# Head-by-head copies out of PSUM in the chunked gated delta rule of a two-layer network

## Chip, core and metric

The kernel runs on one core of a Trainium2 chip. The metric is the device time of one execution in microseconds (us), as the median of several runs. Profiles are of one execution each.

## What is computed

The reference is a two-layer network on x of shape (2, 1024, 256): causal attention with 32 heads of 8, a gated FFN with int8 weights, then a gated delta rule with 16 heads of 128, then an FFN with sign weights; after each a residual and a layer norm. The change touches only the delta rule. Its core, per head and time step, is:

```python
err = jnp.einsum('bhvk,bhk->bhv', S, kt) - vt
S = at[..., None, None] * S - bt[..., None, None] * err[..., None] * kt[:, :, None, :]
o = jnp.einsum('bhvk,bhk->bhv', S, qt)
```

with S a 128 x 128 state for each of 2 x 16 heads, 1024 steps, k scaled by 128 ** -0.5, and q, k, v each made by a projection of x, a causal convolution over 4 steps and a silu. The outputs o are normalised over a head's 128 values, gated, and projected back to 256 columns.

## The kernel before

The recurrence is worked in chunks of 128 time steps. A half sequence has 512 steps (HT), so four chunks (HC = 4); two heads are taken together (HP = 2, a head pair), which makes 8 pairs (NS). With 4 half sequences there are 32 pair steps `i`, each of 4 chunks: 128 chunks in all.

For one chunk of one pair, `recur` (line 488) does this for both heads h, whose results stand side by side in one PSUM tile (a "bank" of 512 float32 columns, made by `bank`, line 129; head h has columns 128h to 128h+127, the slice `r`):

- **rows**, lines 517 and 521: `pr` = transpose of v plus k times the state M, two products for each head, started by the transpose and added to by the second. The second is left out where there is no state yet.
- line 523: ScalarE copies both heads' rows, 256 columns, into SBUF as `prs`.
- **solution**, line 529: `pw` = the chunk's inverted triangular matrix `lt` times `prs`, one product for each head.
- line 531: ScalarE copies both heads' solutions, 256 columns, into SBUF as `wc`.
- **new state**, line 541: `pm` = `kc` times `wc`; VectorE makes the new M from it and the old one (lines 545 and 547).
- **outputs**, lines 554 and 555: `po` = q times the old M plus `at` times `wc`; ScalarE copies them out as `o` (line 558).

All of these products are of float32 data and have 128 output columns for each head. `pr`, `pw`, `pm` and `po` come in turn from one pool of two banks, `pools["c"]`.

Beside the recurrence of pair i, `merge` (line 663) mixes in generators for other work: `keys(i + 4)` (the projection, convolution and Gram matrix of k), `others` (the same for q and v, products of k and q), `rest_of` (gates), `levels` and `blocks` (the inversion of the triangular matrices), `finish` (normalisation and output projection, called through `tail`), and in the last pair steps the FFN of the second layer. Each generator yields numbers that say how much TensorE time has been spoken for, and `merge` takes the one that is furthest behind. That gives the order in which instructions are recorded. When the program is built the framework's scheduler (line 1446, `schedule_with_timeline_sim=True`) places each engine's instructions once more, by their dependences and its own idea of their times; it also puts in the semaphore waits. On the chip each engine takes its instructions strictly in the placed order. A wait of a product therefore holds up all that stands behind it on TensorE.

TensorE's other work in this stage, by line: projections (lines 790 to 792, `pp`, 512 columns, and `pf`, 256 columns), Gram matrices (253, 404), transposes (395, 458), and the levels of the inversion (325 to 380). ScalarE's other work: lines 209, 213 and 223 (convolution and silu), 343 to 381 (levels), 422, 449 and 460 (gates and normalisation).

Of the kernel before, what the change touches and what calls it, by code (L numbers as in the profile page):

```python
# [11 lines left out]
F32 = mybir.dt.float32  # L12
# [8 lines left out]
P = 128  # L21
# [10 lines left out]
HP = 2  # L32
# [56 lines left out]
def delta_rule(  # L89
# [13 lines left out]
    nc = tc.nc  # L103
# [6 lines left out]
    pools = {}  # L110
# [18 lines left out]
    def bank(pool, tag, name):  # L129
        return pool.tile([P, HT], F32, name=name, tag=tag)  # L130
# [47 lines left out]
    def place(i):  # L178

        return divmod(i, NS)  # L180
# [307 lines left out]
    def recur(i):  # L488

        hi, s = place(i)  # L490
        ge = halves[hi]["ge"]
        M = state[s] if hi % 2 else None
        wo = []
        for part in range(2):
            t = pools["late"].tile([P, HP, E], F32R, name=f"wo{part}", tag=f"wo{part}", bufs=1)
            nc.sync.dma_start(
                out=t.bitcast(F32),
                in_=w1d["o", part][s * HP * P : (s + 1) * HP * P, :].rearrange("(h p) e -> p h e", p=P),
            )
            wo.append(t)  # L500

        def tail():
            while tails:
                w = next(tails[0], None)
                if w is not None:
                    return w
                tails.pop(0)
            return 0.0

        lt = st[i]["lt"]  # L510
        o = pools["late"].tile([P, HC, HP, P], F32, name="o", tag="o")
        for c in range(HC):
            t = slice(c * P, (c + 1) * P)
            pr = bank(pools["c"], "c", "pr")
            for h in range(HP):
                r = slice(h * P, (h + 1) * P)
                nc.tensor.matmul(
                    pr[:, r], lhsT=st[i]["v", h][:, t], rhs=ident, start=True, stop=(M is None), is_transpose=True
                )
                if M is not None:  # L520
                    nc.tensor.matmul(pr[:, r], lhsT=st[i]["k", h][:, t], rhs=M[:, r], start=False, stop=True)
            prs = pools["late"].tile([P, HP * P], F32, name="prs", tag="prs")
            nc.scalar.copy(prs, pr[:, 0 : HP * P])  # L523
            yield 0.65
            yield tail()
            pw = bank(pools["c"], "c", "pw")
            for h in range(HP):
                r = slice(h * P, (h + 1) * P)
                nc.tensor.matmul(pw[:, r], lhsT=lt[:, h * HC + c, :], rhs=prs[:, r], start=True, stop=True)  # L529
            wc = pools["late"].tile([P, HP * P], F32, name="wc", tag="wc")  # L530
            nc.scalar.copy(wc, pw[:, 0 : HP * P])  # L531
            yield 0.45
            yield tail()
            Mn = None
            if hi % 2 == 0 or c < HC - 1:
                pm = bank(pools["c"], "c", "pm")
                keep = dict(tag="S", bufs=NS) if c == HC - 1 else dict(tag="M")
                Mn = pools["late"].tile([P, HP * P], F32, name="M", **keep)
                for h in range(HP):
                    r = slice(h * P, (h + 1) * P)  # L540
                    nc.tensor.matmul(pm[:, r], lhsT=st[i]["kc", h][:, c, :], rhs=wc[:, r], start=True, stop=True)  # L541
                for h in range(HP):
                    r = slice(h * P, (h + 1) * P)
                    if M is None:
                        nc.vector.tensor_copy(Mn[:, r], pm[:, r])
                    else:
                        nc.vector.scalar_tensor_tensor(
                            Mn[:, r], M[:, r], ge[:, s * HP + h, c : c + 1], pm[:, r], ALU.mult, ALU.add
                        )
            po = bank(pools["c"], "c", "po")  # L550
            for h in range(HP):
                r = slice(h * P, (h + 1) * P)
                if M is not None:
                    nc.tensor.matmul(po[:, r], lhsT=st[i]["q", h][:, t], rhs=M[:, r], start=True, stop=False)  # L554
                nc.tensor.matmul(  # L555
                    po[:, r], lhsT=st[i]["at", h][:, t], rhs=wc[:, r], start=(M is None), stop=True
                )
            nc.scalar.copy(o[:, c, :, :].rearrange("p h t -> p (h t)"), po[:, 0 : HP * P])  # L558
            M = Mn
            if i == last and c in (HC // 2 - 1, HC - 1):  # L560
                tails.append(finish(i, wo, o, range(c + 1 - HC // 2, c + 1)))
            yield 1.3
            yield tail()
        state[s] = M
        if i < last:
            tails.append(finish(i, wo, o, range(HC)))
# [114 lines left out]
    for i in range(-AHEAD, last + 1):  # L681
# [19 lines left out]
        if i >= 0:  # L701
            parts.append((recur(i), RECUR))
# [747 lines left out]
```

## Time and profile before

| what | us |
|---|---|
| median of 3 runs (2094.62 to 2099.72) | 2094.68 |
| the profiled execution | 2099.4 |
| its span, first to last instruction | 2097.7 |
| the stretch with the recurrence in it, from 837 to 2033 us | 1196 |
| TensorE busy in that stretch | 1127.43 |
| VectorE busy in it | 965.91 |
| ScalarE busy in it | 658.57 |
| GpSimd busy in it | 501.71 |

The profile names engines PE (TensorE's products), PEld (its weight loads, which run beside products), DVE (VectorE), ACT (ScalarE), POOL (GpSimd) and SP (the queue that issues most DMAs). A group's row reads: line, engine, operation, output<-inputs, shapes, count | busy time in us, mean ns of one | idle time of the engine just before them, and what ended it. A float32 product with 128 columns shows as two MATMUL records, so the 256 products of line 529 are x512; a float32 transpose shows as one. Consecutive MATMUL records overlap: four of them that start 0.11 us apart show as one row of 0.60 us. The waits view lists who waited for whom, with total us, number of times and the longest.

### The profile page before, as it was taken

What the parts mean: (1) busy time and instruction counts of PE and PEld (TensorE: products, weight loads), DVE (VectorE), ACT (ScalarE), POOL (GpSimd) and SP (SyncE); (2) the same over time, 40 slices, a digit from 0 to 9 for tenths busy, and PEclk for the clock granted to TensorE, in tenths of its full rate; (3) what the DMA queues carried; (4) which work ended last, traced back from release to release, by engine and by line L of the source; (5) the groups of instructions that cost most, each with busy time, mean ns of one, the idle gap of its engine ahead of it and who ended that gap; (6) DMA issues with size and microseconds to landing.
All of it is one profiled execution on the core that took longest, in us unless ns stands there. A gap on an engine that the chain in (4) does not pass through costs nothing.

```text
span 2097.7 us, 48705 instructions
## 1 busy us (share of the span) xinstructions
PE 1905.9 (91%) x18656; PEld 1498.2 (71%) x18656; DVE 1611.1 (77%) x3878; ACT 1131.9 (54%) x2349; POOL 762.8 (36%) x1217
## 2 busy tenths in 40 slices
PE   4989999999988887899999999999999999999996
PEld 2545555555555786788888888888888888787885
DVE  5756666877747996587788878888898888978587
ACT  2355566576655345555555555655564565555543
POOL 1243333331123322144363443444345344344331
PEclk9899999999999899999999999999999999999999
DMA  7454443442132421443444444443444343443110
GB/s 222 144 164 144 144 131 126 142 134 68 51 75 61 133 64 35 127 126 91 119 121 115 124 118 115 107 120 107 121 131 119 113 118 107 137 118 107 32 41 31
DMA packets 313514, 230.90 MB, mean 110 GB/s; under 512 B 139649, under 2 KB 278657, under 8 KB 313281
## 3 DMA queue, kind: packets, MB, share of 16 engines
q1 hardware_dynamic: 299472, 210.80, 34.6%
q10 hardware_dynamic: 9632, 10.76, 1.6%
q0 software_dynamic: 4176, 6.23, 1.2%
q8 instruction: 147, 2.41, 0.5%
q14 instruction: 87, 0.70, 0.1%
HBM read 172.95 MB, written 51.87 MB: 107 GB/s over the span
## 4 chain that ended last, share of the span: by engine, by line
PE 50%; DVE 19%; ACT 6%; DMA 5%; issue 4%; SPq 1%; POOL 1%; POOLq 0%; DVEq 0%; ACTq 0%
PE pp L790 4%; PE pp L792 4%; PE pp L791 4%; PE ps L1110 4%; PE av L1131 3%; PE ps L1058 3%; DVE q L216 2%; PE pkq L404 2%; DVE at L247 2%; PE pw L529 2%; PE pm L541 2%; DVE k L216 2%; PE pkk L253 2%; PE po L555 2%; PE p L380 2%
## 5 line engine op out<-in xcount | busy, mean ns | idle before, releaser
L1067 DVE TENSOR_REDUCE mx<-ps 128x4 f32<-128x1024 f32 (+1 forms) x320 | 344.7, 1111 | 133.5 <-PE ps L1058 91.9
L1114 ACT ACTIVATE es<-ps 128x512 f32<-128x512 f32 (+1 forms) x608 | 314.8, 577 | 135.3 <-PE ps L1110 128.7
L1110 PE MATMUL ps<-qT,kT 128*128 128x512 f32 (+3 forms) x768 | 221.1, 369 | 17.9 <-ACT es L1114 15.8
L1058 PE MATMUL ps<-kT,qT 128*128 128x512 f32 x576 | 203.2, 428 | 23.3 <-DVE mx L1067 16.9
L1110 PEld LDWEIGHTS ps<-qT,kT 128*128 128x128 f32 x768 | 130.9, 189 | 106.2 <-ACT es L1114 53.7
L216 DVE SCALAR_TENSOR_TENSOR k<-pp,cw,k 128x511 f32<-128x511 f32 (+2 forms) x192 | 141.8, 740 | 31.0 <-ACT k L209 19.9
L1058 PEld LDWEIGHTS ps<-kT,qT 128*128 128x128 f32 x576 | 102.5, 194 | 85.7 <-DVE mx L1067 51.9
L1131 PE MATMUL av<-es,vaug 128*32 128x512 f32 (+3 forms) x1536 | 161.7, 501 | 0.0
L216 DVE SCALAR_TENSOR_TENSOR v<-pp,cw,v 128x511 f32<-128x511 f32 (+2 forms) x192 | 141.2, 738 | 13.1 <-ACT halos L213 8.5
L416 POOL TENSOR_TENSOR q<-q,dg 128x512 f32<-128x512 f32 x64 | 82.2, 1285 | 184.5 <-ACT pt L460 31.6
L216 DVE SCALAR_TENSOR_TENSOR q<-pp,cw,q 128x511 f32<-128x511 f32 (+2 forms) x192 | 139.2, 733 | 11.0 <-ACT q L209 9.4
L740 POOL TENSOR_TENSOR wfl<-wf,wfh 128x256 fp32r<-128x256 f32 x80 | 58.4, 733 | 208.3 <-ACT wfh L828 165.2
L1117 POOL TENSOR_SCALAR_AFFINE_SELECT es<-es 128x512 f32<-128x512 f32 x128 | 80.3, 636 | 146.9 <-ACT es L1114 146.7
L529 PE MATMUL pw<-prs,lt 128*128 128x128 f32 x512 | 84.8, 288 | 23.4 <-ACT prs L523 23.3
L555 PE MATMUL po<-wc,at 128*128 128x128 f32 x512 | 98.4, 279 | 2.1 <-ACT wc L531 1.2
L763 POOL TENSOR_TENSOR om<-om 128x8 f32<-128x8 f32 x93 | 20.3, 218 | 213.7 <-DVE om L756 113.8
L529 PEld LDWEIGHTS pw<-prs,lt 128*128 128x128 f32 x512 | 70.7, 194 | 33.2 <-ACT prs L523 29.7
L558 ACT COPY o<-po 128x256 f32<-128x256 f32 x128 | 47.6, 372 | 79.3 <-PE po L555 78.4
L242 POOL TENSOR_SCALAR_AFFINE_SELECT d<-col 128x512 f32<-128x512 f32 x64 | 51.2, 812 | 105.6 <-DVE at L247 96.7
L554 PE MATMUL po<-M,q 128*128 128x128 f32 x448 | 87.6, 278 | 0.0
L828 ACT CAST wfh<-wf 128x256 fp32r<-128x256 f32 x80 | 32.3, 406 | 101.6 <-DMA wf<-in_w1k 28.6
L531 ACT COPY wc<-pw 128x256 f32<-128x256 f32 x128 | 47.5, 371 | 72.7 <-PE pw L529 71.7
(305 smaller groups left out, 5646.1 us busy)
## 6 DMA issues: line engine op xcount, KB each, us to landing
da<-dec SPq DMA_DIRECT2D x64, 256.0 KB
wk<-w1k SPq DMA_DIRECT2D x64, 256.0 KB
wq<-w1q SPq DMA_DIRECT2D x64, 256.0 KB
wv<-w1v SPq DMA_DIRECT2D x64, 256.0 KB
dg<-dec SPq DMA_DIRECT2D x64, 256.0 KB
wg<-w1g SPq DMA_DIRECT2D x64, 256.0 KB
wo<-w1o SPq DMA_DIRECT2D x64, 256.0 KB
ad<-avs ACTq DMA_DIRECT2D x32, 256.0 KB
```

The costliest lines, as they stand in the source:

```text
L216: nc.vector.scalar_tensor_tensor(acc[:, d:], pp[:, 0 : HT - d], cw[:, n, hd, KS - 1 - d : KS - d], acc[:, d:], ALU.mult, ALU.add)
L529: nc.tensor.matmul(pw[:, r], lhsT=lt[:, h * HC + c, :], rhs=prs[:, r], start=True, stop=True)
L554: nc.tensor.matmul(po[:, r], lhsT=st[i]["q", h][:, t], rhs=M[:, r], start=True, stop=False)
L555: nc.tensor.matmul(po[:, r], lhsT=st[i]["at", h][:, t], rhs=wc[:, r], start=(M is None), stop=True)
L790: nc.tensor.matmul(out, lhsT=lhi, rhs=rhi, start=k0, stop=False)
L791: nc.tensor.matmul(out, lhsT=lhi, rhs=rlo, start=False, stop=False)
L792: nc.tensor.matmul(out, lhsT=llo, rhs=rhi, start=False, stop=k1)
L1058: anchor["mm"] = nc.tensor.matmul(ps[:, j - j0, :].rearrange("p (g k) -> p g k", k=P), lhsT=q_, rhs=kT[:, :, j * P : (j + 1) * P], start=T ...
L1067: nc.vector.tensor_reduce(mx[:, it, j0 // 2, :], ps[:, 0:n, :].rearrange("p j (g k) -> p g j k", k=P), AX.XY, ALU.max)
L1110: nc.tensor.matmul(ps[:, g - g0, :], lhsT=kT[:, g, jb * P : (jb + 1) * P], rhs=qT[:, i0 : i0 + w], start=True, stop=True,)
L1114: exps.append(nc.scalar.activation(es[:, g0 : g0 + n, 0:w], ps, AF.Exp, scale=D ** -0.5))
L1131: mm = nc.tensor.matmul(av[ROW * g : ROW * (g + 1), i0 - ih * 512 : 512], lhsT=vaugs[b][:, jb, kv, :], rhs=es[:, g, 0:w], start=(jb == 0), ...
```

## The change

Both copies of a chunk are cut in two. Each head's half of the rows is copied as soon as its own products are recorded, before the other head's products are recorded; the same is done for the solutions. The tiles `prs` and `wc` are made before the loops. Products, their operands and their number are the same.

```diff
+
             pr = bank(pools["c"], "c", "pr")
+            prs = pools["late"].tile([P, HP * P], F32, name="prs", tag="prs")
             for h in range(HP):
                 r = slice(h * P, (h + 1) * P)
                 nc.tensor.matmul(
...
                 if M is not None:
                     nc.tensor.matmul(pr[:, r], lhsT=st[i]["k", h][:, t], rhs=M[:, r], start=False, stop=True)
-            prs = pools["late"].tile([P, HP * P], F32, name="prs", tag="prs")
-            nc.scalar.copy(prs, pr[:, 0 : HP * P])
+                nc.scalar.copy(prs[:, r], pr[:, r])
             yield 0.65
             yield tail()
             pw = bank(pools["c"], "c", "pw")
+            wc = pools["late"].tile([P, HP * P], F32, name="wc", tag="wc")
             for h in range(HP):
                 r = slice(h * P, (h + 1) * P)
                 nc.tensor.matmul(pw[:, r], lhsT=lt[:, h * HC + c, :], rhs=prs[:, r], start=True, stop=True)
-            wc = pools["late"].tile([P, HP * P], F32, name="wc", tag="wc")
-            nc.scalar.copy(wc, pw[:, 0 : HP * P])
+                nc.scalar.copy(wc[:, r], pw[:, r])
             yield 0.45
             yield tail()
```

In the changed kernel the rows' transposes stand on line 519, the state's products on 523, the two copies on 524 and 532, the solution on 531, the new state on 542 and the outputs on 555 and 556.

## The prediction

> **What bounds the kernel now.** I read the busy shares by engine first, then the stretch with the recurrence, then TensorE's waits in it, then one such wait in order of time.
>
> ```profile
> span 2097.7 us, 48705 instructions
> PE 1905.9 (91%) x18656; PEld 1498.2 (71%) x18656; DVE 1611.1 (77%) x3878; ACT 1131.9 (54%) x2349; POOL 762.8 (36%) x1217
> PE   4989999999988887899999999999999999999996
> ACT  2355566576655345555555555655564565555543
> 837.00:2033.00 1196.00, 1127.43 (x13684) 994.88 (x13684) 965.91 (x2654) 658.57 (x1392) 501.71 (x847) 0.98 0.40 111
> ```
>
> The 128 chunks lie between 837 and 2033 us (first and last row of line 523 in the trace). There TensorE is busy 1127 of 1196 us (94%), VectorE 81%, ScalarE 55%, and the granted clock is 0.98. TensorE's in-order stream sets the end: what adds idle time to it is paid, unless another wait shrinks for it.
>
> ```profile
> PEld pw L529 <- ACT prs L523: 29.7, 29, 9.0
> PEld pm L541 <- ACT wc L531: 14.6, 22, 0.9
> PEld pp L790 <- DVE q L216: 10.7, 14, 1.6
> PEld p L360 <- ACT n L356: 5.9, 6, 2.7
> PEld pp L790 <- DVE k L216: 4.4, 6, 1.1
> PEld po L555 <- ACT wc L531: 2.2, 5, 0.5
> ```
>
> These are waits in that stretch. The two copies cost 29.7 + 14.6 + 2.2 = 46.5 us in 56 places. One of 9.0 us is the first chunk's, where the copy itself was late behind VectorE; without it 37.5 us in 55 places. All other waits of the weight loads there sum to 74.1 us.
>
> ```profile
> 1077.01 0.60 PE L529 MATMUL pw<-prs,lt 128*128 128x128 f32 x4
> ...
> 1077.65 0.37 ACT L531 COPY wc<-pw 128x256 f32<-128x256 f32 x1 [2.40 <-PE pw L529]
> ...
> 1078.07 0.52 PEld L541 LDWEIGHTS pm<-wc,kc 128*128 128x128 f32 x4 [0.65 <-ACT wc L531]
> 1078.07 0.71 PE L541 MATMUL pm<-wc,kc 128*128 128x128 f32 x4 [0.46 <-ACT wc L531]
> ```
>
> A bare stop looks like this. Four records 0.11 us apart from 1077.01 would let the next go at 1077.45; it goes at 1078.07, so 0.62 us of TensorE is lost: 0.20 until the copy starts, 0.37 of copy, 0.05 back.
>
> **The change, part by part.** Products: same kind and number, so no TensorE work is added or removed. Copies: 256 of 256 columns (372 ns each) become 512 of 128 columns. No row shows a 128-column copy out of PSUM. Nearest rows:
>
> ```profile
> L523 ACT COPY prs<-pr 128x256 f32<-128x256 f32 x128 | 47.6, 372 | 37.8 <-PE pr L521 23.6 <-DVE pi L300 7.3 <-PE pr L517 6.0
> L213 ACT COPY halos<-pp 128x3 f32<-128x3 f32 x96 | 14.6, 152 | 0.0
> L338 ACT COPY X<-px 32x512 f32<-32x512 f32 x16 | 9.2, 577 | 0.2
> ```
>
> The price lies between 152 (3 columns) and 372 ns (256); the slopes between these rows, 0.80 and 0.87 ns a column, give 261 to 270, and I take 265. ScalarE then does 512 x 0.265 - 256 x 0.372 = +40 us, going from 659 to 699 us of 1196; it has over 40% idle there, so by itself this costs nothing. Were a ScalarE instruction always queued ahead, its neighbours would be 0.16 us later per chunk and copy kind.
>
> Whether halves overlap is decided by the waits. The built order of the changed program has, in one chunk (lines of the changed kernel):
>
> ```
> L523 pr<-M,k      first head
> ...
> L519 pr<-ident,v  second head   waits ScalarE
> L523 pr<-M,k      second head
> L531 pw<-prs,lt   first head
> ...
> L531 pw<-prs,lt   second head   waits ScalarE
> L542 pm<-wc,kc    first head
> L542 pm<-wc,kc    second head   waits ScalarE
> ```
>
> The second head's transpose into `pr` reads nothing that ScalarE made just then; its semaphore value is that of the first head's copy out of the same bank. That holds in 126 of 128 chunks with a wait on that transpose itself, and for `pw` in 127. So a half's copy does not stand beside the other half's products: the product waits for the copy. Where the old chunk made TensorE stop at two points (before `pw`, before `pm`), the new one can stop at three: before the second `pr`, the second `pw`, the second `pm`. The first `pw` and first `pm` no longer wait.
>
> A rule of the Trainium skill speaks against the change here: "PSUM — Partial Sum Buffer", section "PSUM bank collisions raise a hardware error", says that two engines must not touch one PSUM bank (within 32 partitions) at once, even at disjoint columns, and that access is to be guarded by bank and not by address. The trace of before cannot show this, since its copies start after both heads' products. By the rule the waits must stay and the sum below holds; without it the first rival's 2068 us would.
>
> How often does a stop bite? The scheduler puts other products between. I went through both placed orders and summed, between the product that feeds a copy and the one that waits for it, the spacings of the trace's rows (0.23 us for 512 columns, 0.12 for 256, 0.22 for a float32 product of 128, 0.11 for a transpose). What is short of the bare stop is lost: 0.63 us before, 0.63 - 0.105 = 0.525 after.
>
> - Before: rows 25 places, 13.5 us; solution to new state 23 places, 13.2; solution to outputs 6 places, 2.1. Sum 28.8 us in 54 places.
> - After: first rows to second rows 42 places, 19.5 us; first solution to second solution 40 places, 17.8; second solution to new state 35 places, 9.9 (a `pm` stands between as cover); others 15 places, 2.8. Sum 50.0 us in 132 places.
>
> The waits view shows 37.5 us in 55 places where the count gives 28.8 in 54. The places agree; the size is 1.30 times as large because a copy sometimes finds ScalarE occupied. With the same factor 50.0 becomes 65.0, and the change costs 65.0 - 37.5 = +27.5 us.
>
> Bounds: without the factor +21.2. At 152 ns a copy each of about 120 bare stops is 0.11 us cheaper, which makes +10 with the factor; at 372 it is 0.107 dearer, +44. The other placed work moves a little too (the levels' wait of line 380 on line 376 comes to 4.1 us by the same count, from 0.4; the last FFN's of line 656 to 2.9 from 5.2), which cancels. VectorE's waits for ScalarE (19.9 us for line 209's k is the largest) may grow by the 40 us of copies or shrink as TensorE slows; I take nothing for both. DMA issues, memory and clock are unchanged. What is queued behind the new stops is everything on TensorE, first the projections, whose products VectorE and ScalarE take next. ScalarE's own queue gets a stop as well: the second half's copy waits for the second product, which waits for the first half's copy, and behind it stand lines 209 and 223, which feed VectorE; the factor is my only price for that.
>
> Sum against its own execution: 2099.4 + 27.5 = 2126.9. That execution is 4.7 us above the median, so as a median 2094.7 + 27.5 = 2122 us.
>
> **Rivals.**
>
> *Copies really run beside products.* Then a first half's copy (0.525 us) has 0.33 us of second rows, or 0.22 of second solution, in front of the next need: 0.19 or 0.30 lost where 0.63 was. That saves 0.44 x 25 + 0.33 x 29 = 20.6, by the factor 26.7: 2068 us. For it: the diff's text. Against it: the placed waits in practically every chunk.
>
> *Stops are dearer.* Three round trips through ScalarE's in-order queue each chunk catch more occupied moments: line 523's copies waited 1.07 to 1.9 us in all in a few places of the trace. If every stop costs what the slower ones do (about 0.35 us more than bare), the same count gives 98 after against 48 before, +50: 2145 us. For it: the factor 1.30 was seen with two stops and less ScalarE work. Against it: 45% idle on ScalarE.
>
> *The stops hide in other waits; this is the other side.* TensorE's 74.1 us of other waits, above all line 790's on VectorE's convolution (10.7 + 4.4), shrink by up to one us for each us that TensorE is late. If 27.5 of the 74.1 go, the time is 2095; from 33.8 on the kernel is over 0.3% faster, and at half of them (37) it gives 2085. For it: VectorE is 81% busy and would catch up. Against it: most of those waits are short and at other places than the new stops, and VectorE's input comes through TensorE, so it slows as well.
>
> **How the numbers follow.** About 0.3% (6.3 us) is what a measurement of this kernel can tell from no change. Forecast, three stops at some 0.5 us, +10 to +44: 0.68. Dearer stops: 0.15. Hidden in other waits, within 6.3 us: 0.08; beyond it, faster: 0.05. Real overlap: 0.04. That makes slower 0.83, same 0.08, faster 0.09. The predicted time is 2122 us; the range 2099 to 2148 leaves out the fast cases and most of the no-change case below, and the far end of the dear case above.
>
> **What would show it.** In the changed profile: waits of `pr` on ScalarE's `prs` and of `pw` on `wc`, each about 20 to 28 us in some 40 places, neither of which existed; `pm` on `wc` down to some 13; 512 copies of 250 to 280 ns; TensorE busy and its record count the same within 1%; the 1196 us stretch longer by some 27 us and the others as before. Wrong would be: rows of a copy that lies inside the other head's products of the same bank; other waits of TensorE down by 20 us or more; or copies over 330 ns.

## The result and the profile after

The changed kernel takes 2174.01 us (median of 4 runs, 2168.95 to 2175.58) against 2094.65 us before (4 runs, 2094.33 to 2099.72). The ratio is 1.0372, with a 95% interval from 1.0353 to 1.0391. The profiled execution has a span of 2172.8 us against 2097.7, so 75.1 us have to be found.

The page of the changed kernel, first its head and some of its rows of slices:

```profile
span 2172.8 us, 48999 instructions
PE 1945.1 (90%) x18656; PEld 1519.6 (70%) x18656; DVE 1602.7 (74%) x3878; ACT 1161.7 (53%) x2605; POOL 762.9 (35%) x1217
PE   4899999999997887889999999999988989998996
ACT  2365566666662454555555565465554455555543
PEclk9899999999998998999999999999989999999998
```

The clock row of the kernel before (tenths of full speed in 40 slices), to compare:

```profile
PEclk9899999999999899999999999999999999999999
```

The windows view of the changed kernel from 837 us, as before, to the last chunk's outputs (length, busy time of PE, PEld, DVE, ACT and POOL with instruction counts, then the granted clock):

```profile
837.00:2122.00 1285.00, 1180.98 (x13748) 1024.15 (x13749) 973.16 (x2702) 694.42 (x1655) 503.74 (x850) 0.97 0.37 104
```

TensorE does the same 18656 records, yet shows 39 us more of busy time, in part because a record lasts longer where the clock is lower. ScalarE has 256 instructions more. The recurrence, whose last copy of outputs ended at 2032.5 us, now ends at 2123.0, which is 90 us later; the part behind it is 15 us shorter.

The waits of TensorE's weight loads in that stretch of the changed kernel (total us, times, longest):

```profile
PEld pr L519 <- ACT prs L524: 30.8, 43, 1.8
PEld pw L531 <- ACT wc L532: 22.8, 37, 2.0
PEld pm L542 <- ACT wc L532: 11.7, 33, 0.8
PEld px L335 <- issue: 9.6, 11, 2.4
PEld pp L791 <- DVE q L216: 8.3, 18, 0.8
PEld p L373 <- ACT lt L368: 7.5, 7, 1.6
```

The first two rows did not exist before: the second head's products wait for the first head's copy. One such stop of the changed kernel in order of time:

```profile
1161.86 0.39 PE L523 MATMUL pr<-M,k 128*128 128x128 f32 x2
1161.92 0.37 ACT L559 COPY o<-po 128x256 f32<-128x256 f32 x1 [1.47 <-PE po L556]
...
1162.28 0.27 ACT L524 COPY prs<-pr 128x128 f32<-128x128 f32 x1
...
1162.60 0.14 PEld L519 LDWEIGHTS pr<-ident,v 128*128 128x128 f32 x1 [0.55 <-ACT prs L524]
1162.60 0.33 PE L519 MATMUL pr<-ident,v 128*128 128x128 f32 x1 [0.36 <-ACT prs L524]
1162.60 0.36 PEld L523 LDWEIGHTS pr<-M,k 128*128 128x128 f32 x2
```

The first head's last record starts at 1161.97; without a wait the second head's transpose would go 0.11 us later. It goes at 1162.60, when the copy has ended (1162.28 + 0.27): 0.52 us of TensorE are lost, and there is no product beside the copy. (ScalarE was also busy with the outputs' copy of line 559 until the half copy started.) In the whole trace, none of the 256 copies of rows lies beside a product of lines 519 or 523, and none of the 256 copies of solutions beside one of line 531. The copies themselves, by their groups:

```profile
L532 ACT COPY wc<-pw 128x128 f32<-128x128 f32 x256 | 68.2, 267 | 57.7 <-PE pw L531 57.0
L524 ACT COPY prs<-pr 128x128 f32<-128x128 f32 x256 | 68.1, 266 | 81.2 <-PE pr L523 65.6 <-DVE pi L300 7.3 <-PE pr L519 6.1
```

Where the 75.1 us of the span went, from three views of each trace:

| part | before, us | after, us | difference |
|---|---|---|---|
| weight loads' waits for the copies `prs` and `wc`, without the first chunk's (9.0 and 8.9) | 39.5 | 73.0 | +33.5 |
| loss by the clock, span x (1 - granted clock): 2097.7 x 0.027 and 2172.8 x 0.037 | 56.6 | 80.4 | +23.8 |
| the rest | | | +17.8 |

The first row takes all waits that name the two copies, among them smaller ones (of lines 380 and 555, for instance) beside those of the lists shown. The clock is given to three digits, so its row is good to some 1.5 us. The rest lies in TensorE's other waits: all waits of the weight loads from 820 us on that don't name the two copies sum to 93.0 us before and to 113.4 after. Those of line 335, for instance, went from 5.0 to 9.6 us.

How idle time and clock stand to each other is seen in three adjoining windows of the changed kernel (length, busy time of PE, PEld, DVE, ACT, POOL, then the clock):

```profile
1336.09:1339.50 3.41, 0.88 (x6) 0.69 (x6) 1.91 (x6) 1.69 (x4) 2.89 (x8) 1.00 0.00 0
1339.50:1346.30 6.80, 6.15 (x22) 5.25 (x23) 3.58 (x8) 5.99 (x14) 2.48 (x3) 0.50 0.25 80
1346.30:1349.70 3.40, 3.40 (x82) 3.11 (x81) 2.95 (x5) 2.48 (x5) 0.17 (x1) 1.00 0.24 39
```

After a stretch of 3.41 us in which TensorE was busy for 0.88 us, the clock is at half for 6.8 us. In order of time the projections there look like this:

```profile
1341.58 0.63 PE L793 MATMUL pp<-x2h,wv 128*128 128x512 f32 x1
1342.00 0.63 PE L791 MATMUL pp<-x2h,wv 128*128 128x512 f32 x1
1342.43 0.63 PE L792 MATMUL pp<-x2l,wv 128*128 128x512 f32 x1
```

They start 0.43 us apart, where they are 0.23 apart at the full clock. Such half-clock time within the recurrence sums to 38 us in 7 pieces before and to 83 us in 16 pieces after.

Was the idle time ahead of these falls that of the new stops? In the window above it was not: a transpose waited for GpSimd. Ahead of the fall at 1291.70 us it was: ScalarE came to the copy only at 1291.30, behind other work. In order of time, with the idle time of TensorE before each in brackets:

```profile
1291.62 0.54 PE L531 MATMUL pw<-prs,lt 128*128 128x128 f32 x1 [1.85 <-ACT wc L532]
...
1338.58 0.55 PE L458 MATMUL pt<-ident,o 128*128 128x128 f32 x3 [2.69 <-POOL o L452]
```

In the changed kernel 15 falls begin in the recurrence. In the 3.41 us ahead of each, TensorE's idle time sums to 26.6 us; 7.0 us of it ended with one of the two copies. In 5 of the 15 windows that is the larger part, and these 5 falls hold 27 of the 83 us at half clock. Before the change 6 falls begin there, and 1.3 of 9.9 us ended with the copies, the larger part in none. So by this count the stops stand ahead of about half of the added falls; the others stand behind waits for other work.

### The profile page after: what moved, and what is told of

Its sections match the earlier page's. It is cut to its first block, busy times and chain, and to the rows that moved or that the text cites. A ratio compares the mean times of both kernels' runs of the same rounds, so it can differ in the third digit from the quotient of the medians.

```text
span 2172.8 us, 48999 instructions
## 1 busy us (share of the span) xinstructions
PE 1945.1 (90%) x18656; PEld 1519.6 (70%) x18656; DVE 1602.7 (74%) x3878; ACT 1161.7 (53%) x2605; POOL 762.9 (35%) x1217
## 4 chain that ended last, share of the span: by engine, by line
PE 51%; DVE 16%; ACT 8%; DMA 5%; issue 4%; SPq 2%; POOL 1%; DVEq 0%; POOLq 0%; ACTq 0%
PE pp L791 4%; PE pp L793 4%; PE pp L792 4%; PE ps L1111 3%; PE av L1132 3%; DVE q L216 3%; PE ps L1059 3%; PE pkq L404 2%; DVE at L247 2%; PE pm L542 2%; PE pw L531 2%; DVE k L216 2%; PE pkk L253 2%; PE po L556 2%; PE po L555 2%
## 5 line engine op out<-in xcount | busy, mean ns | idle before, releaser
L531 PE MATMUL pw<-prs,lt 128*128 128x128 f32 x512 | 107.4, 292 | 15.9 <-ACT wc L532 15.6
L524 ACT COPY prs<-pr 128x128 f32<-128x128 f32 x256 | 68.1, 266 | 81.2 <-PE pr L523 65.6
L519 PE MATMUL pr<-ident,v 128*128 128x128 f32 x256 | 74.9, 293 | 32.8 <-ACT prs L524 30.5
L531 PEld LDWEIGHTS pw<-prs,lt 128*128 128x128 f32 x512 | 81.9, 196 | 27.3 <-ACT wc L532 23.5
L542 PE MATMUL pm<-wc,kc 128*128 128x128 f32 x448 | 95.5, 296 | 5.2 <-ACT wc L532 1.3
L532 ACT COPY wc<-pw 128x128 f32<-128x128 f32 x256 | 68.2, 267 | 57.7 <-PE pw L531 57.0
```

## The experiments

The theory: the built program lets no product into a bank from which a ScalarE copy has still to read, so each split copy puts a stop between the heads (a bank stop), and the stops bring a lower clock and later waits with them. The rivals: the 40 us of extra work on ScalarE delay its neighbours; or the changed program was merely placed in an unlucky order. All runs stood beside runs of the kernel before on the same chip.

### The same halves, copied after both heads' products

```diff
# the kernel before, with
-            nc.scalar.copy(prs, pr[:, 0 : HP * P])
+            for h in range(HP):
+                r = slice(h * P, (h + 1) * P)
+                nc.scalar.copy(prs[:, r], pr[:, r])
...
-            nc.scalar.copy(wc, pw[:, 0 : HP * P])
+            for h in range(HP):
+                r = slice(h * P, (h + 1) * P)
+                nc.scalar.copy(wc[:, r], pw[:, r])
```

> Same 512 half copies as the changed kernel (ScalarE about +40 us), but recorded after both heads' products, so no product of the second head waits for the first head's copy. Theory (bank stops, which bring a lower clock and more waits with them): the placed order has 29.2 us of bare copy stops against 28.8 before and 49.8 in the changed kernel, so the time is that of before or up to 10 us over: 2090 to 2105 us. Rival (ScalarE's extra work delays its neighbours): near the changed kernel, 2160 to 2180 us.

2126.23 us, ratio 1.0161 (1.0146 to 1.0176). Neither range held it: 32 us over the kernel before, and 48 under the changed one. The clock is nearly back (loss 59.5 us), the waits for the copies are at 44.4 us. So the interleaving with the products, not the 512 copies, makes the larger part of the loss; the smaller part needed the reshuffles below.

### One of the two copies alone

The changed kernel with the solutions (first run) or the rows (second run) copied whole as before (the tile of the whole copy is made after the loop again, which the diff does not show):

```diff
# rows only
-                nc.scalar.copy(wc[:, r], pw[:, r])
+            nc.scalar.copy(wc, pw[:, 0 : HP * P])
# solutions only
-                nc.scalar.copy(prs[:, r], pr[:, r])
+            nc.scalar.copy(prs, pr[:, 0 : HP * P])
```

> Only the rows' copy is cut and recorded head by head; the solutions are copied whole, as before. Theory (bank stops): placed stops of the copies 52.2 us against 49.8 in the changed kernel, as the solution's stops are unrelieved, so most of the loss is there: 2140 to 2175 us. Rival (ScalarE's extra work, half of it here): 2130 to 2137 us. Additive view (each part half): about 2134 us.

> Only the solutions' copy is cut and recorded head by head; the rows are copied whole. Theory (bank stops): placed stops 51.6 us, with 20.3 us of other placed stops against 11.6 before, so 2140 to 2180 us. Rival (ScalarE's extra work, half of it here): 2130 to 2137 us. Additive view: about 2134 us, and the losses of the two parts sum to 79 us.

Rows only: 2158.39 us, ratio 1.0311 (1.0281 to 1.0341). Solutions only: 2176.36 us, ratio 1.0390 (1.0373 to 1.0407). Both lie in the theory's ranges. Each part alone costs about what both cost (65 and 83 us against 79); the two losses sum to some 148 us and not to 79. The waits of rows only:

```profile
PEld pm L542 <- ACT wc L532: 27.6, 42, 1.2
PEld pr L519 <- ACT prs L524: 26.2, 40, 1.6
PEld pw L530 <- ACT prs L524: 18.4, 40, 1.2
```

And of solutions only:

```profile
PEld pw L531 <- ACT prs L524: 29.3, 39, 1.5
PEld pw L531 <- ACT wc L532: 29.3, 50, 1.2
...
PEld pm L542 <- ACT wc L532: 13.0, 33, 0.8
```

Here the number of stops is read off. The old chunk has two (before `pw`, before `pm`). Splitting either copy makes three. Splitting the other as well adds a stop between its heads but takes the one of the whole copy away, so there are three again. By this count what is paid for is the third stop, and the first split brings it.

### A bank for each head

The changed kernel, with the bank taken inside the loop, so that each head's rows and each head's solution have one of their own:

```diff
-            pr = bank(pools["c"], "c", "pr")
             for h in range(HP):
                 r = slice(h * P, (h + 1) * P)
+                pr = bank(pools["c"], "c", "pr")
...
-            pw = bank(pools["c"], "c", "pw")
             for h in range(HP):
                 r = slice(h * P, (h + 1) * P)
+                pw = bank(pools["c"], "c", "pw")
```

> The changed kernel with each head's rows and each head's solution in a PSUM bank of its own, so that a copy and the other head's product no longer share one. Same copies, same ScalarE work. Theory (bank stops): placed copy stops 29.8 us, and 9.5 us of waits of the next rows for the outputs' copy against 1.4 before, since the two banks are passed round faster: 2085 to 2115 us. Rival (ScalarE's extra work, or interleaving heads as such): 2160 to 2180 us.

2117.68 us, ratio 1.0118 (1.0092 to 1.0143): 56 us better than the changed kernel with the same products, the same 512 copies and the heads interleaved as there, though 3 us over the range. Its waits (one entry of 8.9 us is the first chunk's):

```profile
PEld pw L531 <- ACT prs L524: 23.3, 34, 8.9
PEld pp L791 <- DVE q L216: 18.2, 24, 1.9
PEld pm L542 <- ACT wc L532: 15.4, 34, 0.8
PEld pr L519 <- ACT o L559: 11.6, 20, 1.0
```

No second head waits for the first head's copy; the copies' waits are 32.8 us in all, under the 39.5 of the kernel before. In their place comes the next chunk's `pr` behind the copy of the outputs (11.6 us), because the two banks are passed round six times a chunk where it was four. With a bank for each head, 59 of the 256 copies of rows lie beside a product of lines 519 or 523, and 55 of the 256 copies of solutions beside one of line 531; in the changed kernel none did. The shared bank is the cause of the stops: this is shown.

### What a mere reshuffle costs, and what ScalarE's work costs

Two runs change one planning number of the kernel before, which moves only the order of instructions (14 shown; 13.1 in the other). A third adds two tiny copies to each chunk that nobody waits for:

```diff
# reshuffles: the share of the recurrence
-KEYS, OTHERS, FIRST_OTHERS, RECUR, GATES, LEVELS, TAIL = 9.685, 11.658, 15.197, 12.328, 3.1, 24.4, 1.711
+KEYS, OTHERS, FIRST_OTHERS, RECUR, GATES, LEVELS, TAIL = 9.685, 11.658, 15.197, 14, 3.1, 24.4, 1.711
# extra work for ScalarE
             nc.scalar.copy(prs, pr[:, 0 : HP * P])
+            nc.scalar.copy(pools["late"].tile([P, 4], F32, name="sc", tag="sc"), prs[:, 0:4])
...
             nc.scalar.copy(wc, pw[:, 0 : HP * P])
+            nc.scalar.copy(pools["late"].tile([P, 4], F32, name="sd", tag="sd"), wc[:, 0:4])
```

> The kernel before with one planning number changed (the share of time that the mixing of generators gives to the recurrence, 12.328 to 14), which changes nothing but the order of instructions; placed copy stops 28.6 us against 28.8. It measures what a mere reshuffle costs. Theory (bank stops make most of the loss, reshuffling a lesser part of it): 2085 to 2115 us. Rival (placement alone made the loss: the order before was the best found and any other is far worse): 2130 us or more.

> As the run before, with 13.1 in place of 14; placed copy stops 29.2 us. Theory: 2085 to 2115 us. Rival (placement alone): 2130 us or more.

> The kernel before, and after each of its two whole copies of a chunk one more ScalarE copy of 4 columns that nobody waits for: 256 more instructions of some 155 ns, about 40 us of ScalarE, as in the changed kernel; placed copy stops 28.2 us. Rival (ScalarE's extra work is what late halves paid for): 2120 to 2135 us. Theory (reshuffling by itself gives such sums): within the spread of the two reshuffles, 2085 to 2115 us.

At 14: 2112.58 us, ratio 1.0106 (1.0077 to 1.0135). At 13.1: 2111.67 us, ratio 1.0095 (1.0069 to 1.0122). The small copies: 2096.55 us, ratio 1.0036 (1.0016 to 1.0057). So the order of the kernel before is worth about 20 us over two others with the same work, and 256 more ScalarE instructions cost about 5 us (12 at most, by the interval). With that, most of the 32 us of the late halves and of the 24 us of the two banks can be what leaving that order costs. This is argued and not shown: the small copies moved TensorE's order as well (2725 of its 18656 records have another tile at their place, against 5446 at 14) and lost only 5 us.

### The changed kernels in other orders

The changed kernel at 14 and at 13.1, and the two-bank kernel at 14:

> The changed kernel with the same planning number at 14: another order, the same bank stops (placed copy stops 51.3 us, others 15.9 against 11.6). Theory (bank stops): the loss stays, 2160 to 2190 us. Rival (the changed kernel's order was an unlucky one): back to 2095 to 2140 us.

> The changed kernel with the planning number at 13.1; placed copy stops 51.4 us, others 12.1. With runs of both kernels at 12.328, 13.1 and 14 the change is seen at three orders. Theory (bank stops, with their consequences, are worth the same in any order): 60 to 90 us over the old kernel at 13.1, so 2170 to 2200 us. Rival (some 20 us of the loss are only the old kernel's lucky order, which the changed kernel at other orders need not pay again): 2150 to 2170 us.

> The kernel with a bank for each head's rows and solution, with the planning number at 14; placed copy stops 30.6 us, others 16.1. Theory: no bank stops, so it stands within 15 us of the old kernel at 14, 2100 to 2130 us. Rival (interleaving the heads costs by itself): 2140 us or more.

| planning number | before | changed | bank for each head |
|---|---|---|---|
| 12.328 (as given) | 2094.65 | 2174.01 | 2117.68 |
| 13.1 | 2111.67 | 2161.36 | not run |
| 14 | 2112.58 | 2196.15 | 2112.14 |

The ratios to the kernel before are 1.0513 (1.0480 to 1.0546) for the changed kernel at 14, 1.0320 (1.0302 to 1.0338) at 13.1, and 1.0099 (1.0075 to 1.0122) for two banks at 14. At the same number the change costs 79, some 50 and 84 us. At 14 the changed kernel is 6 us above the theory's range. At 13.1 the time lies in the rival's range, and the loss is 30 us smaller than in the order as given. At 14 the two-bank kernel equals the old one (2112.14 against 2112.58), and the shared bank makes 84 us, together with the order that the scheduler gives each of the two kernels.

### Two attempts on the stops themselves

In the first, other generators' work is recorded between the heads. In the second, the first head's half is copied twice, so that each stop is longer by one copy.

```diff
# other work between (rows; the same for the solutions with 0.225)
                 nc.scalar.copy(prs[:, r], pr[:, r])
-            yield 0.65
+                yield 0.325
+                if h == 0:
+                    yield tail()
# longer stops (rows; the same for the solutions)
+                if h == 0:
+                    nc.scalar.copy(pools["late"].tile([P, P], F32, name="sc", tag="sc"), pr[:, r])
                 nc.scalar.copy(prs[:, r], pr[:, r])
```

> The changed kernel, with other generators' work recorded between the first and the second head of rows and solutions, which gives the second head's products cover. Placed copy stops 48.2 us in 127 places against 49.8 in 132, so the scheduler hardly uses it. Theory (what the placed order shows decides): 2160 to 2195 us, no real gain. Rival (the recorded order decides): 2110 to 2150 us.

> The changed kernel with the first head's half copied twice, once into a scratch tile and then into place, for rows and for solutions: a bank stop is longer by one copy (0.266 us). Placed copy stops 67.4 us against 49.8, by the factor 1.3 some 23 us more. Theory (a stop brings a lower clock and later waits with it): more than the 23 us, 2200 to 2230 us, with a longer time at the half clock. Rival (a stop costs only itself, or hides): 2174 to 2197 us with the same time at the half clock.

Other work between: 2166.55 us, ratio 1.0346 (1.0330 to 1.0361), waits for the copies 70.6 us against 73.0. The scheduler's placing decides, and it left nearly as many stops. Longer stops: 2191.43 us, ratio 1.0458 (1.0429 to 1.0488), 17 us over the changed kernel, in the rival's range. Its waits for the copies are 79.9 us against 73.0, so 7 us more where 23 were priced, and its clock loss is 71.9 against 80.4; the profiled execution is the fastest of four, 10 us below the median, and the other three lost 70 to 88 us by the clock. So this run does not show that a longer stop brings the clock down further; with another order again, it does not refute it either.

All profiles together, sorted by whether the second head waits for the first head's copy:

| kernel | span | waits for copies | clock loss |
|---|---|---|---|
| before; at 14; at 13.1; small copies | 2097.7; 2110.4; 2101.4; 2095.7 | 39.5; 40.8; 42.4; 38.4 | 56.6; 63.3; 50.4; 54.5 |
| late halves; two banks; two banks at 14 | 2124.4; 2124.0; 2107.1 | 44.4; 32.8; 34.3 | 59.5; 59.5; 59.0 |
| changed; at 14; at 13.1; work between | 2172.8; 2197.8; 2158.9; 2167.4 | 73.0; 74.7; 74.6; 70.6 | 80.4; 94.5; 73.4; 88.9 |
| rows only; solutions only; longer stops | 2149.9; 2178.0; 2179.4 | 75.2; 73.9; 79.9 | 66.6; 84.9; 71.9 |

Every kernel with bank stops has 70 us or more of waits for the copies and over 66 us of clock loss; no kernel without them is over 45 and 64. Over all executions, and not the profiled ones alone, the clock losses meet: 46 to 72 us without bank stops, 65 to 104 with them. Among the kernels with bank stops the clock loss doesn't follow the waits for the copies: rows only has 75.2 us of waits and 66.6 of clock loss, work between 70.6 and 88.9. None of these kernels beats the one before.

## Why the prediction was wrong

The direction and the mechanism of the stops were right; the size was far off, outside the range: +79 us where +27.5 was forecast. Two terms that the sum put at nothing make more than half of the loss.

- *The waits on the shared bank* hold, as the order of the built program showed, and no half copy ran beside a product of its kind. The bank-for-each-head run shows that the shared bank is their cause.
- *A bare stop of 0.525 us, a copy of 265 ns*: measured 0.52 us and 266 to 267 ns.
- *The number of stops and their size*: 42, 40, 35 and 15 places were counted; the waits view shows 43 for the second rows, 37 for the second solution, 33 for the new state. With the factor 1.30 they were to cost 25.4, 23.1, 12.9 and 3.6 us; the three rows of the view give 30.8, 22.8 and 11.7. The sum of 65.0 was to stand against 37.5; by all waits that name the copies it is 73.0 against 39.5. The term +27.5 was +33.5.
- *"DMA issues, memory and clock are unchanged"*: this is the step that failed first. The clock loss rose by 23.8 us. The forecast priced the idle time that the stops add, but not the half clock that followed such time. The added stops stand ahead of 5 of the 15 falls, which hold 27 of the 83 us at half clock; the other falls stand wholly or mainly behind other waits, so only a part of this term belongs to the stops themselves.
- *"The other placed work moves a little too ... which cancels"*, and *"I take nothing for both"*: the other failed step. The two waits that it named did nearly cancel (line 380 on line 376 went from 0.7 to 2.8 us, the last FFN's of line 656 from 3.8 to 2.1), but some 18 us lie in waits that don't name the two copies. The two reshuffles of the old kernel cost about as much, so leaving the old order can be enough to make such a sum. How much of the 18 us is the order and how much follows from the stops stays open: the changed kernel itself moves by 35 us between orders.
- *ScalarE's 40 us more cost nothing by themselves*: nearly right, the small copies show about 5 us, 12 at most.
- *The rivals*: "copies really run beside products" was wrong for the stated reason. "Dearer stops" came nearest in time but not in cause: the waits cost 0.54 us each on average (73.0 us in 134 places), not much dearer than the 0.49 priced (65.0 in 132) and far from the rival's 0.74 (98 in 132; by the 0.35 us that it adds to each place, its 98 would be 96). "The stops hide in other waits" had the wrong sign: the other waits grew.
- *The stretch*: line 523's last copy starts at 2024.9 us; what ends at 2033 is the last copy of outputs. Nothing in the sum hangs on that. The stretch ends 90 us later and not 27, and TensorE's busy time by 2% and not within 1%.

## What to carry to other kernels

With both halves in one PSUM bank, no product of rows or solutions ran beside a copy of its kind; cutting a copy in halves gave overlap only where the halves lay in different banks, and in one bank it traded two waits for three. Even with the overlap no order tried was faster than the kernel before. On a TensorE that is over 90% busy, price an added stop at its length, and leave room for the clock: here 24 us beside 34, of which the stops themselves account for a part. In a kernel whose order has been tuned, give any edit that makes the scheduler place it anew some 20 us (1%) of uncertainty to the slow side (three such edits that left the stops as they were cost 5, 20 and 21 us), and test an edit at several orders before judging it.

## What the runs showed of the hardware beside that

TensorE's clock fell to half without TensorE standing idle for a whole window of 3.41 us. Before each of the 15 falls that begin in the recurrence of the changed kernel, TensorE was idle for 0.7 to 2.5 us of the last 3.41 us, by the ends that the profile models; the median of such windows has no idle time at all. Before the change there were 6 such falls, behind 1.0 to 2.1 us of idle time. A fall lasts 3.4, 6.8 or 10.2 us. Cut into such windows, in step with the falls, the changed kernel's recurrence has 13 at full clock with 1.5 us of idle time or more, and 11 of them were followed by a fall; before it was 5 of 8. With less than 0.7 us of idle time none was, in either. This matches "TensorE: Matmul & The Clock Gate" of the Trainium skill, section "Part 1: The HAM clock gate (the "warmup" mystery)", in the two clock levels and in the window of some 3.4 us; but its table of the two states puts the half clock after at least one idle window, and here windows that were busy for a quarter to four fifths of their length were followed by the half clock. That idle time is the cause is argued from this order of events; no run changed the one without the other.
